# First layer's experts: an earlier flag for the branch, and later weight sums beside lone tiles

## Chip, cores and metric

The kernel runs on one core of a Trainium2 chip. The metric is the time of one execution on the device in microseconds, as the median of several runs. The engines are PE (TensorE, matrix products; its weight loads are listed as PEld), DVE (VectorE), ACT (ScalarE), POOL (GpSimd) and SP (SyncE, which here starts most DMAs). Each engine runs its own list of instructions in order and waits on semaphores for the others.

## What is computed

Two layers, each a graph convolution followed by a mixture of experts, on 3327 tokens of 256 features, in float32. `adj` is sparse: some 0.24% of its entries and the diagonal are not zero.

```python
# layer 0
x = x + relu(adj @ (layernorm(x) @ W) + b)
x = x + moe0(layernorm(x))      # 8 experts, 2 per token, hidden size 1024, relu
# layer 1
x = x + gnn1(layernorm(x))      # the 700 largest of tanh(adj * adj) in each row; tanh, relu
x = x + moe1(layernorm(x))      # 8 experts, 2 per token, hidden size 256, gelu; out = tokens + sum
```

For each chosen expert `e` of layer 0, a token gets `combine[e] * (relu(t @ W1[e].T + b1[e]) @ W2[e].T + b2[e])`.

## The kernel before

**Blocks of layer 0's experts.** Tokens are scattered into lists by expert, and the experts work through blocks: a pair is two tiles of 128 tokens of one expert, a lone tile is one. Blocks are numbered t = 0 to 29 and more if the data ask for it. Among t = 3 to 24 ("piped") the lone tiles are t = 12, 17 and 22. SP loads each block's tokens, weights and biases into a ring of six places, two for a block, so that a block's loads start about two blocks ahead of it.

**Seven products for eight.** A product of two by two halves is made with seven partial products instead of eight, after sums of the operands have been formed (the Strassen-Winograd scheme). This holds for pairs in both of an expert's products. The sums of the second product's weights `w2` are `t1, t2, t4, t3` (L1350, four VectorE operations of 128x512 that write the tile `gate`); those of its hidden activations are `s1, s2, s4, s3` (L1447, L1448, L1451, L1478). The sums of the first product's weights `w1` are made by POOL (L1532, L1533, L1535) and, one of them, by VectorE (L1515); those of its tokens by VectorE (L1544, L1547, L1548). A lone tile takes plain products.

**A period.** `piped_step(t)` works on two blocks at once: the first product of block t + 1 (`first_parts`, seven parts, products on L1586) alternates with the second product of block t (`second_parts` for a pair, products on L1435; `single_parts` for a lone tile, L1714). For i = 0 to 6 it lists part i of the first, then part i of the second, and between them what `after_first(i)` and `after_second(i)` hold. Part 2 of the first product adds a partial product into the hidden activations' quarter `c11` (L1609 on VectorE) and ACT applies bias and relu (L1594); part 3 ends with ACT's copy of a PSUM bank into `c12` (L1614), and part 5 accumulates into that bank, so it waits for the copy. L1622 adds into `c22`, and part 7 ends with the addition into `c12` (L1632); the relu of `c12` follows in the next period. In the next period the parts of block t + 1's second product follow: x_1, b_, z_1, x_2, z_2, x_3, q_. Their results are weighed and added to the output tile by VectorE (L1442, L1497). z_1 multiplies `s1` with `t1`, x_2 `s2` with `t2`, x_3 `s3` with `t3`, and q_ takes `t4`.

While period t runs, the four weight sums of block t + 1's second product (`nexts`) are listed one by one behind parts of block t, in the order that the dictionary gives:

```python
if i in (2, 3, 5, 6):
    nexts[{2: 0, 3: 1, 5: 3, 6: 2}[i]]()
```

**What sets the order on an engine.** The program is listed once; a scheduler then orders each engine's instructions: of those whose inputs it reckons ready, the one listed first goes first. `behind(x)` adds that what is listed inside it goes on its engine after the instruction x. The order is fixed when the program is built.

**The branch.** Before block 26 the kernel branches (`tc.If(first_usual > 0)`, L2233) on whether the usual counts of tokens hold. `usual()` (from L1140) forms the flag: one small PE product (L959), seven small VectorE operations (L961, L1147, L1148, L1150, L1154 twice, L1161), and then `nc.values_load`, in which each engine reads the flag from SBUF into a register (L1162). The call stands behind block 25, `layer0.step(late, place=...)`. A second such branch, in layer 1, forms its flag by the same function. In the usual arm SP loads outputs of earlier blocks (L1832), and blocks 26 to 29 follow. Blocks 25 and 26 are not piped: their weight sums are listed by `prepare` (L1353, behind the last operation on the output tile), the first product is L1385, and L1376 makes one of the sums of the activations.

Of the kernel before, what the change touches and what calls it, by code (L numbers as in the profile page):

```python
# [14 lines left out]
ALU = mybir.AluOpType  # L15
# [12 lines left out]
E = 8  # L28
# [7 lines left out]
TOPK = 700  # L36
# [28 lines left out]
FIXED = (4, 6)  # L65
# [14 lines left out]
BEGUN, FIRST_TILES, MORE_TILES = 12, 14, 22  # L80
# [48 lines left out]
def gnn_moe_two_layers(  # L129
# [24 lines left out]
    nc = tc.nc  # L154
# [31 lines left out]
    def blk(name, n):  # L186

        at = blk_places[name][blk_at[name] % len(blk_places[name])]
        blk_at[name] += 1
        return pad[:, at : at + n]  # L190
# [103 lines left out]
    def behind(instructions):  # L294

        if instructions and any(i is instructions[-1].ins for i in nc.cur_bb.bb.instructions):
            return tc.issue_after(instructions[-1].ins)
        return nullcontext()
# [657 lines left out]
    def tokens(routed, name="pl_cnt"):  # L956

        pc = pst.tile([P, E], F32, name="pc", tag="pt")
        nc.tensor.matmul(pc, lhsT=ones_sq, rhs=cum[:, routed, :], start=True, stop=True)  # L959
        cnt = work.tile([P, E], F32, name=name, bufs=1)  # L960
        nc.vector.tensor_copy(cnt, pc)  # L961
        return cnt
# [177 lines left out]
    def usual(covered, small, tier=None):  # L1140


        most = work.tile([P, 1], F32, name="pl_most", bufs=1)
        ok = work.tile([P, 1], F32, name="pl_ok", bufs=1)
        for i, (tiles, rows_) in enumerate(covered):
            cnt = tokens(tiles, "pl_first_cnt")
            nc.vector.tensor_tensor(cnt, cnt, rows_, ALU.is_gt)  # L1147
            nc.vector.tensor_reduce(most, cnt, AX.X, ALU.max)  # L1148
            if i == 0:
                nc.vector.tensor_scalar(ok, most, -1.0, 1.0, ALU.mult, ALU.add)  # L1150
            else:
                nc.vector.scalar_tensor_tensor(ok, most, 0.5, ok, ALU.is_le, ALU.mult)
        for number, limit in small:
            nc.vector.scalar_tensor_tensor(  # L1154
                ok[0:1, :], number, float(limit), ok[0:1, :], ALU.is_le, ALU.mult
            )
        if tier is not None:
            nc.vector.tensor_reduce(most, tier, AX.X, ALU.min)
            nc.vector.tensor_tensor(ok, ok, most, ALU.mult)
        flag = work.tile([P, 1], I32, name="pl_flag", bufs=1)  # L1160
        nc.vector.tensor_copy(flag, ok)  # L1161
        return nc.values_load(flag[0:1, 0:1], min_val=0, max_val=1)  # L1162

    def places(cnt, nb, base, size, starts_, n, at, table, own, aside):
# [51 lines left out]
    def experts(xlist, ys, group, fixed, n_hidden, func, w1T, b1, w2T, b2, copy, order_of_places, kept=None,  # L1216
# [49 lines left out]
        def groups_of(t):  # L1266
            return SG if t < EARLY or order[t - EARLY] < LATE_PAIRS else 1
# [64 lines left out]
        def halves(a, k, i):  # L1332
            return a[:, k * hc_n // 2 : (k + 1) * hc_n // 2, ts(i, P)]
# [169 lines left out]
                return [x_1, q_, b_, z_1, x_2, z_2, x_3]  # L1503
            return [x_1, b_, z_1, x_2, z_2, x_3, q_]

        weight_sums, owed_sums, owed_relu, begun_y = [], [], [], {}
        token_sums, hidden, ahead_sums = {}, {}, {}

        def quarter(w1, k, d):
            n = n_hidden // 2  # L1510
            return w1[:, d, k * n : (k + 1) * n]
# [39 lines left out]
        def first_parts(t):  # L1551

            _, _, w1, bb1, _, _ = loaded[t]
            xT = ready.pop(t)
            hT = blk("wide", hc_n * SB).rearrange("p (c b) -> p c b", b=SB)
            hidden[t] = hT
            hn = hc_n // 2

            if groups_of(t) < SG:
                def some(at):  # L1560
                    for hc in range(at, at + 2):
                        ps = psh.tile([P, P], F32, name="ps_h", tag="ph")
                        for c in range(DC):
                            last_product[:] = [nc.tensor.matmul(
                                ps, lhsT=w1[:, c, ts(hc, P)], rhs=xT[:, c, :], start=(c == 0),
                                stop=(c == DC - 1),
                            )]
                        last_hidden[:] = [nc.scalar.activation(
                            hT[:, hc, 0:P], ps, func, bias=bb1[:, hc : hc + 1]
                        )]  # L1570
                return [lambda at=at: some(at) for at in range(0, hc_n, 2)]

            s1, s2, s3, s4 = weight_sums[0:4]
            t1, t2, t3, t4 = token_sums.pop(t)
            a11, a12, a21, a22 = (quarter(w1, k, d) for k in range(2) for d in range(2))
            b11, b12, b21, b22 = (xT[:, d, ts(i, P)] for d in range(2) for i in range(2))
            c11, c12, c21, c22 = (halves(hT, k, i) for k in range(2) for i in range(2))
            ps = {}

            def bank(name, pool, tag):  # L1580
                ps[name] = pool.tile([P, hn, P], F32, name="ps_f", tag=tag)
                return ps[name]

            def multiply(out, a, b, first=True):
                for c in range(hn):
                    last_product[:] = [nc.tensor.matmul(  # L1586
                        out[:, c, :], lhsT=a[:, ts(c, P)], rhs=b, start=(first and c == 0),
                        stop=(c == hn - 1), skip_group_check=True,
                    )]

            def relu(k, i, src):
                for c in range(hn):
                    hc = k * hn + c
                    last_hidden[:] = [nc.scalar.activation(  # L1594
                        hT[:, hc, ts(i, P)], src[:, c, :], func, bias=bb1[:, hc : hc + 1]
                    )]

            def part1():
                multiply(bank("b", psh, "ph"), a11, b11)
                with behind(last_hidden):  # L1600
                    d = nc.scalar.copy(c11, ps["b"])
                with tc.issue_after(d.ins):
                    for q in owed_relu:
                        q()
                owed_relu.clear()

            def part2():
                multiply(bank("a", pst, "pt"), a12, b21)
                nc.vector.tensor_tensor(c11, c11, ps["a"], ALU.add)  # L1609
                relu(0, 0, c11)  # L1610

            def part3():
                multiply(ps["b"], s2, t2, False)
                nc.scalar.copy(c12, ps["b"])  # L1614

            def part4():
                multiply(bank("z", pst, "pt"), s1, t1)

            def part5():
                multiply(ps["b"], s3, t3, False)  # L1620
                nc.scalar.copy(c22, ps["b"])
                nc.vector.tensor_tensor(c22, c22, ps["z"], ALU.add)  # L1622

            def part6():
                multiply(ps["b"], a22, t4, False)
                relu(1, 0, ps["b"])
                with behind(last_hidden):
                    relu(1, 1, c22)

            def part7():  # L1630
                multiply(ps["z"], s4, b22, False)
                nc.vector.tensor_tensor(c12, c12, ps["z"], ALU.add)  # L1632
                owed_relu.append(lambda: relu(0, 1, c12))

            return [part1, part2, part3, part4, part5, part6, part7]

        def piped_step(t, late, place):
# [8 lines left out]
            sums = ahead_sums.pop(t, None)  # L1646
            nexts, weights_ = [nothing] * 4, [nothing] * 4
# [28 lines left out]
            def after_second(i):  # L1676
                if owed_sums and i in (1, 2):
                    owed_sums.pop(0)()
                if i in (2, 3, 5, 6):
                    nexts[{2: 0, 3: 1, 5: 3, 6: 2}[i]]()  # L1680

            for i in range(7):
                if first_[i]:
# [299 lines left out]
    with nc.allow_non_contiguous_dma("a few hundred elements"):  # L1983
# [8 lines left out]
    sums = const.tile([1, ng], F32, name="most_sums")  # L1992
    nc.vector.tensor_reduce(sums, pc.rearrange("o (n k) -> o n k", k=NCHUNK), AX.X, ALU.add)
    most_all = const.tile([1, 1], F32, name="most_all")
# [6 lines left out]
    late = plan(positive.rearrange("p n i k -> p (n i k)"))  # L2001
# [2 lines left out]
    layer0.steps_to(late, layer0.always - 5)  # L2004
    in_s = s.rearrange("p n d -> p (n d)")
    at = BEGUN * K * D
    layer0.step(late, place=in_s[:, at : at + DC * SB])

    first_usual = usual(
        [(BEGUN, late[4][:, E : 2 * E])],
        [(late[5][0:1, :], FIXED[0]), (most_all, TOPK + 0.5)],
    )
    before_branch, rows_before = layer0.state(), list(rows_written)
    begun_stats = (
        const.tile([P, BEGUN, 2], F32, name="begun_mv"), const.tile([P, BEGUN], I32, name="begun_rs")
# [213 lines left out]
    with tc.If(first_usual > 0) as arms:  # L2233
# [9 lines left out]
        with behind(last_y):  # L2243
# [10 lines left out]
        layer1.steps_to(late1, EARLY - 1)  # L2254
        layer1.step(late1, place=blk("xT_arms", DC * SB))
        baset, nbt = late1[4], late1[6]
        second_usual = usual(
            [(FIRST_TILES, baset[:, E : 2 * E]), (MORE_TILES, baset[:, 2 * E :])],
            [(late1[5][0:1, :], FIXED[1])],
            nbt[:, E : 2 * E],  # L2260
        )
        before_inner = layer1.state()
        with tc.If(second_usual > 0) as inner:
            layer1.know(2 * E)
# [213 lines left out]
```

## Time and profile before

| what | value |
|---|---|
| median of 8 runs | 1184.1 us (1181.87 to 1188.06) |
| the profiled execution | 1182.32 us, span 1180.6 us |
| granted TensorE clock | 0.988 |
| PE busy | 1131.5 us (96%) |
| VectorE busy | 923.1 us (78%) |
| ACT busy | 652.9 us (55%) |
| POOL busy | 395.7 us (34%) |

The profile is of one execution; the span runs from its first instruction to its last. A line of a timeline reads: start in us, duration in us, engine, source line, operation, output and inputs with sizes, count, and in brackets how long the engine had been idle and for whom it waited. A line of the list of waits reads: who waited for whom, us in total, times, longest. In the chain of waits, each piece is what the end of the execution hung on at that time. Matrix products overlap, and their ends are modelled: in the blocks, a product of 128x128 follows the one before it after 0.11 us while it is listed with 0.28.

### The profile page before, as it was taken

Reading aid. Unit: us, or ns where it says so; the run is one execution under the profiler, and the core shown is the slowest. Engines: PE = TensorE matmul, PEld = TensorE weight load, DVE = VectorE, ACT = ScalarE, POOL = GpSimd, SP = SyncE. Lnnn points to the kernel's source line nnn. Section 1 sums busy time; section 2 is a strip of 40 time slices with the busy share of each in tenths; the row PEclk is TensorE's granted clock in tenths of the full one; section 3 lists DMA queues with packets and bytes.
Section 4 is the critical chain, followed back from the end, with each engine's and each line's share of the span. In section 5 each row is a group of like instructions: output and inputs, shape, how many; then the busy total and the mean of one; then the engine's idle time right before and its main releaser. Section 6 shows DMA issues by size and latency. Waiting matters only on the chain.

```text
span 1180.6 us, 20682 instructions
## 1 busy us (share of the span) xinstructions
PE 1131.5 (96%) x6667; PEld 1010.7 (86%) x6667; DVE 923.1 (78%) x2728; ACT 652.9 (55%) x1309; POOL 395.7 (34%) x424
## 2 busy tenths in 40 slices
PE   8999999999999999999999999999999999988983
PEld 7888888888779999999998988888888888877862
DVE  6698999988868998888876669486798788784464
ACT  5699657550225655555553346989778683133331
POOL 2111331242434543535341110012444324554541
PEclk9999999999999999999999999999999999999997
DMA  9996638724465566676666955135644734557696
GB/s 349 183 266 264 242 122 249 254 78 165 139 203 191 195 229 229 192 251 214 226 231 234 360 195 215 59 116 192 221 145 170 262 122 130 181 166 232 202 295 221
DMA packets 123254, 241.77 MB, mean 205 GB/s; under 512 B 24528, under 2 KB 93184, under 8 KB 116224
## 3 DMA queue, kind: packets, MB, share of 16 engines
q1 hardware_dynamic: 108656, 205.59, 53.3%
q0 software_dynamic: 11200, 31.61, 7.4%
q10 hardware_dynamic: 3280, 3.15, 0.8%
q8 instruction: 55, 0.90, 0.3%
q14 instruction: 63, 0.52, 0.1%
HBM read 203.99 MB, written 36.33 MB: 204 GB/s over the span
## 4 chain that ended last, share of the span: by engine, by line
PE 82%; DMA 6%; DVE 6%; issue 3%; ACT 2%; POOL 1%; SPq 0%; ACTq 0%; DVEq 0%; POOLq 0%
PE ps_g L449 32%; PE ps_y L1435 10%; PE ps_h L1385 8%; PE ps_f L1586 8%; PE ps_y L1747 6%; PE ps_g L756 4%; DMA ring<-in_adjT 3%; PE ps_g L474 3%; PE ptb L1325 2%; PE ps_s L396 2%; PE ps_p L2063 2%; PE ps_o L485 2%; DMA ring<-ys 1%; DVE rt_product L819 1%; DMA x<-in_x 1%
## 5 line engine op out<-in xcount | busy, mean ns | idle before, releaser
L449 PE MATMUL ps_g<-ring,pad 128*128 128x256 f32 x1040 | 235.6, 381 | 1.3 <-DMA ring<-in_adjT 1.3
L449 PEld LDWEIGHTS ps_g<-ring,pad 128*128 128x128 f32 x1040 | 194.9, 190 | 26.9 <-DMA ring<-in_adjT 1.7
L946 POOL DMA_INDIRECT ys<-pad,index x114 | 118.2, 1037 | 196.0 <-DVE pad L1755 58.1
L449 PE MATMUL ps_g<-ring,s 128*128 128x256 f32 x780 | 176.8, 379 | 0.0
L459 DVE TENSOR_TENSOR ring<-ring,ring 128x768 f32<-128x768 f32 (+1 forms) x160 | 167.4, 1088 | 0.0
L449 PEld LDWEIGHTS ps_g<-ring,s 128*128 128x128 f32 x780 | 147.9, 190 | 19.9
L675 ACT ACTIVATE ring<-ring 128x3328 f32<-128x3328 f32 x54 | 160.1, 2976 | 1.2 <-DMA ring<-in_adjT 0.8
L946 POOL DMA_INDIRECT xlist<-xn,rt_idx x104 | 115.2, 1108 | 127.3 <-issue 39.5
L1925 ACT ACTIVATE sign<-ring,below 128x416 bf16<-128x416 f32 x208 | 133.4, 641 | 13.6 <-DMA ring<-in_adjT 7.7
L819 DVE SCALAR_TENSOR_TENSOR rt_product<-xn,gate 128x256 f32<-128x256 f32 x256 | 116.3, 454 | 15.1 <-ACT xn L361 5.6
L1393 ACT ACTIVATE pad<-ps_h,ring 128x256 f32<-128x256 f32 (+1 forms) x114 | 51.6, 455 | 133.9 <-PE ps_h L1385 94.3
L1385 PE MATMUL ps_h<-pad,ring 128*128 128x256 f32 (+1 forms) x512 | 113.9, 370 | 6.7 <-ACT pad L1329 4.1
L1385 PEld LDWEIGHTS ps_h<-pad,ring 128*128 128x128 f32 x512 | 90.3, 193 | 24.3 <-ACT pad L1329 5.6
L1594 ACT ACTIVATE pad<-pad,ring 128x128 f32<-128x128 f32 x216 | 69.0, 398 | 28.3 <-DVE pad L1609 26.8
L474 PE MATMUL ps_g<-ring,s 128*128 128x256 f32 x312 | 68.7, 380 | 3.9 <-ACT s L361 3.9
L474 PEld LDWEIGHTS ps_g<-ring,s 128*128 128x128 f32 x312 | 58.9, 190 | 12.4 <-ACT s L361 4.4
L756 PE MATMUL ps_g<-s,ring 128*128 128x256 f32 x312 | 69.0, 380 | 0.0
L756 PEld LDWEIGHTS ps_g<-s,ring 128*128 128x128 f32 x312 | 58.8, 190 | 7.9
L1442 DVE SCALAR_TENSOR_TENSOR pad<-ps_y,ring,pad 128x128 f32<-128x128 f32 x138 | 47.1, 344 | 15.6 <-PE ps_y L1435 14.2
L929 POOL COPY xn<-rt_w 128x4 f32<-128x4 f32 x26 | 4.6, 200 | 163.2 <-DVE rt_w L892 163.2
L1586 PE MATMUL ps_f<-xn 128*128 128x128 f32 x432 | 56.9, 276 | 2.0 <-ACT pad L1614 2.0
L1532 POOL TENSOR_TENSOR xn<-ring 128x512 f32<-128x512 f32 x18 | 27.9, 1553 | 90.0 <-DMA ring<-in_f_w1T 83.3
(287 smaller groups left out, 2139.7 us busy)
## 6 DMA issues: line engine op xcount, KB each, us to landing
ring<-in_adjT SPq DMA_DIRECT2D x50, 1664.0 KB
ring<-in_f_w1T SPq DMA_DIRECT2D x30, 1024.0 KB
ring<-in_f_w2T SPq DMA_DIRECT2D x30, 1024.0 KB
ring<-xlist SPq DMA_DIRECT2D x52, 258.0 KB
ring<-in_f_w SPq DMA_DIRECT2D x36, 256.0 KB
ring<-ys SPq DMA_DIRECT2D x12, 512.0 KB
ring<-in_f_b SPq DMA_DIRECT2D x34, 128.0 KB
xlist<-h2T SPq DMA_DIRECT2D x16, 257.0 KB
```

The costliest lines, as they stand in the source:

```text
L449: nc.tensor.matmul(ps, lhsT=b[:, c, :], rhs=a[:, c, :], start=(first and c == 0), stop=(c == CJ - 1), skip_group_check=not first,)
L459: nc.vector.tensor_tensor(out[:, part, :], out[:, part, :], other[:, part, :], ALU.add)
L474: nc.tensor.matmul(sums[pan][c], lhsT=s[:, j, ts(c, P)], rhs=piece(pan, j // CJ)[:, j % CJ, :], start=(j == 0), stop=(j == NT - 1),)
L675: last_pass[:] = [nc.scalar.activation(a, a, f)]
L756: nc.tensor.matmul(banks_[it], lhsT=piece(pan, k)[:, c, ts(it, P)], rhs=s[:, j, :], start=(j == 0), stop=(j == NT - 1),)
L819: nc.vector.scalar_tensor_tensor(product, xn, 1.0, gate[:, e, :], ALU.mult, ALU.mult, accum_out=sc[:, e : e + 1],)
L946: d = nc.gpsimd.indirect_dma_start(out=a[:, :], out_offset=bass.IndirectOffsetOnAxis(ap=index, axis=0), in_=rows_, in_offset=None,)
L1385: last_product[:] = [nc.tensor.matmul(ps, lhsT=w1[:, c, ts(hc, P)], rhs=xT[:, c, :], start=(c == 0), stop=(c == DC - 1),)]
L1435: last_product[:] = [nc.tensor.matmul(ps, lhsT=a[:, c, :], rhs=b[:, c, :], start=(first and c == 0), stop=(c == hc_n // 2 - 1), skip_group ...
L1586: last_product[:] = [nc.tensor.matmul(out[:, c, :], lhsT=a[:, ts(c, P)], rhs=b, start=(first and c == 0), stop=(c == hn - 1), skip_group_c ...
L1747: last_product[:] = [nc.tensor.matmul(ps, lhsT=hT[:, hc, ts(g, P)], rhs=w2[:, hc, :], start=(hc == 0), stop=(hc == hc_n - 1),)]
L1925: nc.scalar.activation(sign, piece(pan, k)[:, :, ts(i, GROUP)], AF.Sign, bias=below, accum_out=positive[:, pan, i, k : k + 1],)
```

## The change

It has two parts. First, `usual()` returns the flag's tile, and a new function `is_set()` reads it into the registers. For layer 0 the flag is formed ahead of block 25 and read where it was read before, behind it. For layer 1 both calls stand where the one stood.

Second, in the period of a lone tile (`sums` is empty there) the four weight sums `nexts` are no longer listed behind parts 3, 4, 6 and 7, but all behind part 7, and on VectorE's list after `last_sum`, the addition into `c12` that part 7 of `first_parts` ends with (L1632). In the periods of pairs nothing changes.

```diff
@@ usual
         flag = work.tile([P, 1], I32, name="pl_flag", bufs=1)
         nc.vector.tensor_copy(flag, ok)
+        return flag
+
+    def is_set(flag):
         return nc.values_load(flag[0:1, 0:1], min_val=0, max_val=1)
@@ first_parts
             def part7():
                 multiply(ps["z"], s4, b22, False)
-                nc.vector.tensor_tensor(c12, c12, ps["z"], ALU.add)
+                last_sum[:] = [nc.vector.tensor_tensor(c12, c12, ps["z"], ALU.add)]
                 owed_relu.append(lambda: relu(0, 1, c12))
@@ piped_step
             def after_second(i):
                 if owed_sums and i in (1, 2):
                     owed_sums.pop(0)()
-                if i in (2, 3, 5, 6):
+                if sums and i in (2, 3, 5, 6):
                     nexts[{2: 0, 3: 1, 5: 3, 6: 2}[i]]()
+                if not sums and i == 6:
+                    with behind(last_sum):
+                        for q in nexts:
+                            q()
@@ before the branch of layer 0
-    layer0.step(late, place=in_s[:, at : at + DC * SB])
-    first_usual = usual(
+    usual_flag = usual(
         [(BEGUN, late[4][:, E : 2 * E])],
         [(late[5][0:1, :], FIXED[0]), (most_all, TOPK + 0.5)],
     )
+    layer0.step(late, place=in_s[:, at : at + DC * SB])
+    first_usual = is_set(usual_flag)
@@ before the branch of layer 1
-        second_usual = usual(
+        second_flag = usual(
             [(FIRST_TILES, baset[:, E : 2 * E]), (MORE_TILES, baset[:, 2 * E :])],
             [(late1[5][0:1, :], FIXED[1])],
             nbt[:, E : 2 * E],
         )
+        second_usual = is_set(second_flag)
```

More of the change, by code (lines that the diff above doesn't have):

```diff
@@ L1504, in second_parts @@
             return [x_1, b_, z_1, x_2, z_2, x_3, q_]
-        weight_sums, owed_sums, owed_relu, begun_y = [], [], [], {}
+        weight_sums, owed_sums, owed_relu, last_sum, begun_y = [], [], [], [], {}
         token_sums, hidden, ahead_sums = {}, {}, {}
```

## Prediction

> **What bounds the kernel now.** I read the page first. TensorE is busy 96% of the span at a granted clock of 0.99, so a microsecond is won only where PE stands still. The second view is the list of PE's waits from 440 to 660 us, the stretch of the pipelined blocks of layer 0 and of the branch:
>
> ```profile
> PE   1131.5 (96%) x6667; PEld 1010.7 (86%) x6667; DVE 923.1 (78%) x2728; ACT 652.9 (55%) x1309; POOL 395.7 (34%) x424
> ```
> ```profile
> PE ps_h L1385 <- DVE pl_flag L1161: 2.8, 1, 2.8
> PE ps_f L1586 <- ACT pad L1614: 2.0, 3, 1.1
> PE ps_y L1435 <- DVE xnT L1447: 0.8, 3, 0.4
> ```
>
> These are all of PE's waits there: one at the branch, and two in or just after each of the three lone tiles (t = 12, 17, 22). The change aims at the first and second rows; the third is the one it can make worse. Third, the chain of waits around the branch:
>
> ```profile
> 639.88 0.05 PE pc L959
> ...
> 641.62 0.17 DVE pl_flag L1161
> 641.78 0.88 issue
> 642.66 2.49 PE ps_h L1385 x10
> ```
>
> PE has nothing to do from its last product (next one possible at 639.71) to 642.66, 2.95 us: the flag's small operations stand behind the block's last VectorE work (L1442, until 640.52), and then every engine reads the flag and branches (0.88). Last, VectorE's timeline in the first lone period:
>
> ```profile
> 474.07 0.68 DVE L1350 TENSOR_TENSOR gate<-ring 128x512 f32<-128x512 f32 x1
> ...
> 475.67 0.68 DVE L1350 TENSOR_TENSOR gate<-ring,gate 128x512 f32<-128x512 f32 x1
> 476.27 0.68 DVE L1350 TENSOR_TENSOR gate<-ring 128x512 f32<-128x512 f32 x1
> 476.87 0.68 DVE L1350 TENSOR_TENSOR gate<-ring,gate 128x512 f32<-128x512 f32 x1
> 477.47 0.68 DVE L1609 TENSOR_TENSOR pad<-pad,ps_f 128x512 f32<-128x512 f32 x1
> 481.79 0.69 DVE L1622 TENSOR_TENSOR pad<-pad,ps_f 128x512 f32<-128x512 f32 x1 [3.65 <-ACT pad L1621]
> ...
> 485.76 0.68 DVE L1632 TENSOR_TENSOR pad<-pad,ps_f 128x512 f32<-128x512 f32 x1
> 486.36 0.15 DVE L1409 TENSOR_TENSOR index<-index,positive 128x2 int32<-128x2 f32 x1
> 486.43 0.34 DVE L1442 SCALAR_TENSOR_TENSOR pad<-ps_y,ring,pad 128x128 f32<-128x128 f32 x1
> 487.08 0.69 DVE L1609 TENSOR_TENSOR pad<-pad,ps_f 128x512 f32<-128x512 f32 x1 [0.31 <-PE ps_f L1586]
> 487.79 1.12 DVE L1447 TENSOR_TENSOR xnT<-pad 128x512 f32<-128x512 f32 x1
> ```
>
> The four weight sums (L1350) run ahead of L1609, so c11 is late, then ACT's relu, then its copy L1614, for which PE waits. After that VectorE idles 3.65 us. But behind L1632 it has no room: the table by stages gives it 12.70 busy of 13.00 us from 487 to 500 and 12.93 of 13.00 from 500 to 513, and z_1 starts at 488.96, 0.05 after L1447.
>
> **The flag.** Seven small operations (0.15 to 0.19 us each, 640.44 to 641.78 or 1.34 us in all) and one product (0.17) move ahead of block 25. They have their inputs long before. On VectorE they can delay block 25's weight sums, which end at 629.57 and are first needed by a product at 634.35, and L1376, after which VectorE idles 2.73 us; so 1.34 us is covered (uncovered it would cost at most 1.34). No DMA moves; SP, POOL and ACT only meet their flag reads without a wait, and SP's first transfers in the arm still wait for the block's last scatter, issued at 641.40. What stays on PE is reading and branching: 641.81 to 642.66, 0.85 us. At the second branch PE reads the flag while products are queued, and at 1124.65 a read and eight register steps begin while LDWEIGHTS issue on until 1125.5, so PE's queue reaches at least 0.85 us ahead there. I take 0.2 us left of the 2.95: a gain of 2.75; the ends are 2.95 (fully hidden) and 2.1 (0.85 in the open). VectorE, which also restarts earlier, does so after its last L1442, before it is needed.
>
> [...] The queue of this trace shows no more than about ten instructions ahead.
>
> **The sums behind the activations' sums, first lone period.** What is won: L1609 no longer stands behind three of the sums. It waits for its product, 475.98 + 0.10 = 476.08, ends 476.75; the relu's first three and a part (1.19) let L1614 end at 478.53; PE reaches part5 at 478.48 + 0.86 = 479.34 instead of 479.98. Won: 0.64 (0.56 and 1.29 in the other two, by the same rows: 540.67 - 540.11, 601.80 - 600.51).
>
> What it costs: L1632 now comes earlier too, and behind it the four sums go in one piece, since nothing listed before them is left. The same construction in block 25 shows the order (two L1353, a third, an index operation, the fourth, 626.96 to 629.57). Forward from part5 at 479.34: L1622 481.15, three token sums to 482.82, L1719 to 483.26, L1720 blocked by POOL's L1532 until 484.35, L1632 484.35 to 484.95. Then 4 x 0.60 of sums + 0.33 (L1409, L1442) + 0.60 (L1609) + 0.60 (L1447) = 3.95: 488.90 without POOL. That is already the 488.91 at which L1447 ends now: all that was won is spent. And POOL's own sums of 1.27 us fall into it. What they do to such an operation the trace shows:
>
> ```profile
> 497.03 2.20 DVE L1350 TENSOR_TENSOR gate<-ring 128x512 f32<-128x512 f32 x1
> ```
> ```profile
> 497.38 1.29 POOL L1535 TENSOR_TENSOR xn<-ring,xn 128x512 f32<-128x512 f32 x1
> ```
>
> The weight sum ends 0.56 after POOL's. So L1533 (to 485.57) holds the first sum 0.6, and L1535, from 486.7 behind a scatter, holds the third 1.2: L1447 ends at 490.7, z_1 starts at 490.75 instead of 488.96, **+1.8**. Second lone period, the same way: 551.35 instead of 549.66, **+1.7**. Third, where L1632 gains 2.4 us because PE had waited 1.12 there: 611.65 instead of 610.93, **+0.7**. Behind z_1 VectorE is full for two more blocks (13.17 us from L1447 to L1447, PE's own 12.94), so nothing is caught up. Sum +4.2. Ends for each period: 1.2 less, if POOL's L1535 lets the sums pass, 0.3 more, if b_'s L1442 goes ahead of L1447 too; so +0.6 to +5.1.
>
> [...]
>
> **Sum.** -2.75 + 4.2 = +1.45 us against the profiled execution (1182.3, span 1180.6, 1.7 around it; 1.8 under the median of the runs). On the median of 1184.1: 1185.5, inside the 0.2% (2.4 us) that a measurement of this kernel can tell from no change. Ends: +0.6 - 2.95 = -2.35 and +5.1 - 2.1 = +3.0.
>
> **Rivals.** (1) *The sums find room.* If L1442, L1609 and L1447 go ahead of the sums, z_1 is not delayed and the three waits on L1614 vanish: -0.64 - 0.56 - 1.29 = -2.5, with the flag -5.25: 1178.9. For: VectorE idles 3.65 us in that period now, and z_1 needs only the first sum. Against: idle time lies before L1632, and the sums may not start there any more. (2) *The arm is not at hand.* PE's 2.1 us of standing before the read (639.71 to 641.81) may have covered the fetch of the arm's instructions. Now PE arrives at once; if the fetch takes over 0.85 us it shows, and at 2.1 the flag gains only 0.65: +4.2 - 0.65 = +3.55, 1187.7. For: one branch on PE, at 1159.71, lasts 3.96 us. Against: that one jumps; both branches that fall into an arm take 0.08. (3) *The first half does nothing*, because the sums were ready too late anyway: then L1609 would not stand behind them; the timeline excludes it.
>
> **How the numbers follow.** The forecast's case 0.58: its centre +1.45 with ends -2.35 to +3.0, widened by shifts of the rest of the order, puts 0.23 over +2.4, 0.32 between, 0.03 under -2.4. Rival 1: 0.25, all faster. Rival 2: 0.17, slower. Together faster 0.28, same 0.32, slower 0.40. The range goes from 1178.8, through the middle of rival 1, to 1188.6, past rival 2 and its spread of 1; about 0.13 and 0.04 are left out. The forecast's own range is 1181.7 to 1187.1.
>
> **What would show it.** The wait on pl_flag gone and PE's gap at the branch under 0.5 us; no wait of PE on L1614; the four L1350 in one piece after L1632; PE's waits on L1447 grown from 0.8 us to some 7; POOL's L1535 inside the sums. Wrong if L1447 stands ahead of the sums (rival 1), or PE idles over 1 us between the branch and its next product (rival 2).

## The result and the profile after

The kernel after takes 1188.9 us (median of 24 runs), the kernel before 1183.8 us beside it (66 runs). The ratio is 1.0048, interval 1.0033 to 1.0063, so the change costs 5.7 us (3.9 to 7.5); the two medians lie 5.1 us apart. The forecast was 1185.5 us, +1.45; the range ended at 1188.6, just below the result.

The profiled execution after has a span of 1194.3 us at a clock of 0.979; with 1196.0 us it is one of the kernel's longest. Some 5 us of its distance to the one before arise before 350 us, in code that the change leaves as it was; this does not belong to the change. From 475 us on the two differ by +8.4 us, which can be followed piece by piece. First the page and the list of PE's waits in the stretch of the blocks and of the branch (who waits for whom: us in total, times, longest):

```profile
PE 1140.4 (95%) x6667; PEld 1019.6 (85%) x6667; DVE 925.3 (77%) x2728; ACT 652.7 (55%) x1309; POOL 394.5 (33%) x424
```
```profile
PE ps_y L1438 <- DVE xnT L1450: 9.6, 4, 3.0
PE ps_f L1589 <- DMA ring<-in_f_w1T: 0.8, 1, 0.8
```

(Lines after L1160 have moved by 3, those behind the period's code by 7.) The waits on `pl_flag` and on L1614 are gone. In their place PE waits four times for s1 (L1450, which was L1447): in the periods behind the three lone tiles, 8.2 us together, and in block 28, 1.3 us. VectorE's timeline in the first of these periods, and what POOL does there:

```profile
489.61 0.68 DVE L1635 TENSOR_TENSOR pad<-pad,ps_f 128x512 f32<-128x512 f32 x1
490.20 1.97 DVE L1353 TENSOR_TENSOR gate<-ring 128x512 f32<-128x512 f32 x2
492.10 2.21 DVE L1353 TENSOR_TENSOR gate<-ring,gate 128x512 f32<-128x512 f32 x1
...
494.56 0.67 DVE L1353 TENSOR_TENSOR gate<-ring,gate 128x512 f32<-128x512 f32 x1
495.16 0.67 DVE L1612 TENSOR_TENSOR pad<-pad,ps_f 128x512 f32<-128x512 f32 x1
...
496.02 0.89 DVE L1450 TENSOR_TENSOR xnT<-pad 128x512 f32<-128x512 f32 x1
```
```profile
489.75 1.27 POOL L1536 TENSOR_TENSOR xn<-xn,ring 128x512 f32<-128x512 f32 x1
...
492.46 1.29 POOL L1538 TENSOR_TENSOR xn<-ring,xn 128x512 f32<-128x512 f32 x1
494.85 1.52 POOL L1535 TENSOR_TENSOR xn<-ring 128x512 f32<-128x512 f32 x1 [1.10 <-DMA ring<-in_f_w1T]
```

VectorE's order is the predicted one but for one operation: the four sums stand in one piece behind L1635, POOL's sums fall inside them, and s1 comes last, with a second L1445 ahead of it as well. PE's order has changed too. The kernel before has eight products of the next block in front of z_1, the kernel after has sixteen, so eight products (1.0 us) run before the wait that came after it:

```profile
487.70 1.06 PE L1586 MATMUL ps_f<-xn 128*128 128x128 f32 x8
488.96 1.16 PE L1435 MATMUL ps_y<-gate,xnT 128*128 128x128 f32 x8 [0.20 <-DVE xnT L1447]
```
```profile
491.99 1.95 PE L1589 MATMUL ps_f<-xn 128*128 128x128 f32 x16
496.97 2.07 PE L1438 MATMUL ps_y<-gate,xnT 128*128 128x128 f32 x8 [3.04 <-DVE xnT L1450]
```

What the prediction did not have stands in the table of stretches, which gives for each its length, busy time (and count) of PE, PEld, DVE, ACT and POOL, then the granted clock, the DMA share and GB/s:

```profile
493.22:496.64 3.42, 0.71 (x7) 0.52 (x5) 3.42 (x7) 0.77 (x3) 2.24 (x3) 1.00 1.01 338
496.64:500.05 3.41, 3.08 (x13) 3.04 (x14) 3.38 (x5) 0.98 (x3) 1.41 (x1) 0.50 0.29 102
500.05:503.46 3.41, 3.41 (x32) 3.41 (x32) 3.41 (x9) 1.08 (x2) 0.00 (x0) 1.00 0.02 5
```

PE stands idle for 3.04 us up to 496.97, and then its clock is 0.50 for 3.41 us: 13 products where the next stretch has 32. Behind the second lone tile it is at half for 6.83 us (561.49 to 568.32), behind the third not at all. Product by product against the kernel before, the three periods cost 3.6, 5.9 and 0.6 us, the branch gains 2.95, and block 28 gives 1.3 back. In the second period 0.8 us is the wait for `in_f_w1T` in the list above, which two later profiles of the kernel after do not have.

### The profile page after: what moved, and what is told of

It is laid out like the page before. It is cut to its first block, busy times and chain, and to the rows that moved or that the text cites. A ratio compares the mean times of both kernels' runs of the same rounds, so it can differ in the third digit from the quotient of the medians.

```text
span 1194.3 us, 20678 instructions
## 1 busy us (share of the span) xinstructions
PE 1140.4 (95%) x6667; PEld 1019.6 (85%) x6667; DVE 925.3 (77%) x2728; ACT 652.7 (55%) x1309; POOL 394.5 (33%) x424
## 5 line engine op out<-in xcount | busy, mean ns | idle before, releaser
L1388 PE MATMUL ps_h<-pad,ring 128*128 128x256 f32 (+1 forms) x512 | 117.3, 378 | 7.5 <-ACT pad L1332 4.1
L474 PEld LDWEIGHTS ps_g<-ring,s 128*128 128x128 f32 x312 | 60.1, 194 | 11.5 <-ACT s L361 3.1
L1445 DVE SCALAR_TENSOR_TENSOR pad<-ps_y,ring,pad 128x128 f32<-128x128 f32 x138 | 47.2, 345 | 17.0 <-PE ps_y L1438 15.8
L1438 PE MATMUL ps_y<-gate,xnT 128*128 128x128 f32 x352 | 49.6, 288 | 9.6 <-DVE xnT L1450 9.6
L1535 POOL TENSOR_TENSOR xn<-ring 128x512 f32<-128x512 f32 x18 | 29.8, 1658 | 84.7 <-DMA ring<-in_f_w1T 78.0
```

The lines of the kernel that those rows point to most:

```text
L474: nc.tensor.matmul(sums[pan][c], lhsT=s[:, j, ts(c, P)], rhs=piece(pan, j // CJ)[:, j % CJ, :], start=(j == 0), stop=(j == NT - 1),)
L1388: last_product[:] = [nc.tensor.matmul(ps, lhsT=w1[:, c, ts(hc, P)], rhs=xT[:, c, :], start=(c == 0), stop=(c == DC - 1),)]
L1438: last_product[:] = [nc.tensor.matmul(ps, lhsT=a[:, c, :], rhs=b[:, c, :], start=(first and c == 0), stop=(c == hc_n // 2 - 1), skip_group ...
```

## The experiments

They ran in three groups, each beside runs of the kernel before: 1166.9 us in the first, 1185.9 in the second, 1167.2 in the third. Only ratios within a group are compared. "The clock's part" is (1 - granted clock) x span, the mean over a kernel's runs; it also counts half-clock time in which PE waited anyway.

| kernel | group | ratio to before (interval) | us | clock's part (before) |
|---|---|---|---|---|
| e1_flag | 1 | 0.9993 (0.9978 to 1.0009) | -0.8 | 9.7 (10.5) |
| e2_sums | 1 | 1.0071 (1.0046 to 1.0095) | +8.3 | 13.4 (10.5) |
| e3_c11 | 1 | 0.9983 (0.9963 to 1.0004) | -2.0 | 10.7 (10.5) |
| e4_filler | 1 | 1.0036 (1.0022 to 1.0050) | +4.2 | 9.2 (10.5) |
| p_before | 2 | 1.0002 (0.9980 to 1.0025) | +0.2 | 16.9 (15.7) |
| p_after | 2 | 1.0037 (1.0019 to 1.0055) | +4.4 | 18.2 (15.7) |
| e5_best | 2 | 0.9962 (0.9938 to 0.9985) | -4.5 | 15.0 (15.7) |
| e6_flag_loads | 2 | 0.9940 (0.9921 to 0.9960) | -7.1 | 14.7 (15.7) |
| e7_no_pool | 3 | 0.9964 (0.9946 to 0.9982) | -4.2 | 10.0 (11.0) |
| e8_c11_only | 3 | 0.9978 (0.9958 to 0.9999) | -2.6 | 11.5 (11.0) |
| e9_filler14 | 3 | 1.0026 (1.0009 to 1.0043) | +3.0 | 8.8 (11.0) |
| p_after2 | 3 | 1.0062 (1.0043 to 1.0082) | +7.2 | 14.7 (11.0) |

**Each part alone.** The flag (after, with the sums back in their places), and the sums (before, with `last_sum` and `behind` as in the change):

```diff
# e1_flag, against after
-                if sums and i in (2, 3, 5, 6):
+                if i in (2, 3, 5, 6):
                     nexts[{2: 0, 3: 1, 5: 3, 6: 2}[i]]()
-                if not sums and i == 6: ...
# e2_sums, against after
-        return flag
-    def is_set(flag):
         return nc.values_load(...)      # usual() called and read behind block 25, as before
```

> The flag formed ahead of block 25, the weight sums where they were. Theory (the gain at the branch is partly handed back): PE's gap of 2.95 us at the branch goes whole, but PE stands about 1.3 us in front of block 28's first products of the second half, because VectorE's weight sums of block 28 wait for its w2, which SP's queue brings behind three large loads of outputs. Net -1.65 us, ratio 0.9986, and VectorE's L1353 sums near 680 us show a wait for in_f_w2T of about 1.3 us. Rival (the hand-back belongs to the sums, not to the flag): -2.95 us, 0.9975, no such wait. Rival (the flag itself costs, by fetching the arm's code or by block 25's later sums): PE's gap at the branch stays over 1 us and the ratio is 1.000 or more.

> The weight sums of lone tiles behind the addition into c12, the flag where it was. Theory (delay of s1 and a halved clock behind it): PE's wait on L1614 goes and waits on s1 of 2 to 3 us appear in the three periods; behind those of some 3 us the granted clock is 0.5 for 3.4 us or more, which costs 1.7 us for each 3.4 us; together +7 to +10 us, ratio 1.006 to 1.0085; PE's gap at the branch stays at 2.8. Rival (only the waits count, the halved clock comes and goes with the run as it does in the kernel before): +4 to +5 us, 1.0035 to 1.004, and no half-clock stretch that follows the lone tiles' gaps. Rival (the slower time lies elsewhere, before block 12 or in layer 1): 1.000 to 1.002 with the same gaps.

With the flag alone PE has no idle time over 0.12 us at the branch, but 1.45 us in front of block 28's z_1. VectorE's waits and its timeline there:

```profile
DVE gate L1356 <- DMA ring<-in_f_w2T: 1.4, 1, 1.4
```
```profile
657.04 1.29 DVE L1356 TENSOR_TENSOR gate<-ring 128x512 f32<-128x512 f32 x2 [1.37 <-DMA ring<-in_f_w2T]
...
660.59 5.76 DVE L1849 TENSOR_TENSOR x<-x,s 128x1024 f32<-128x1024 f32 x5
...
666.94 0.69 DVE L1450 TENSOR_TENSOR xnT<-pad 128x512 f32<-128x512 f32 x1
```

Block 28's `w2` has not landed when VectorE, now 2.95 us earlier, wants it; the additions of earlier outputs (L1849) follow without a break, and s1 is late by the same amount. So the hand-back belongs to the flag, against the first rival; and with nothing left of the gap at the branch the second has fallen too. Net by the profile -2.95 + 1.45 = -1.5; measured -0.8 (-2.6 to +1.1), which agrees with the -1.65 expected but does not prove a gain. The sums alone cost 8.3 us (5.4 to 11.1), as the theory said and above the rival's 4 to 5.

**What the lateness of s1 is made of.** In group 3 POOL's three sums in a lone tile's period were left out, with the order on PE and VectorE as in the kernel after; the next block then works with stale sums, so only the times count:

```diff
# e7_no_pool, against after
-                    weights_ = sum_weights(t + 2)
+                    weights_ = sum_weights(t + 2) if sums else [nothing] * 2 + sum_weights(t + 2)[2:3] + [nothing]
```

> The kernel after, in which POOL leaves out its three sums of w1 (L1535, L1536, L1538) that belong to a lone tile's period: nothing else is moved, the block behind reads stale sums. Theory (the four sums and what follows take 4 us by themselves, and POOL's operations in the same microseconds hold VectorE's up by 2 to 4 us more): VectorE's four L1353 run at 0.60 us each, and PE's waits on s1 go from 2 to 3 us in a period to 0 to 1; with no half-clock stretch behind them; 6 to 8 us faster than the kernel after, ratio to the kernel before 0.997 to 0.999. [...]

> The kernel after, unchanged, beside the three others on the same chip: 1.0035 to 1.0055 by both theories, with waits on s1 of 2 to 3 us in the three periods and in most executions one to three half-clock stretches behind them.

VectorE's timeline of the first period, without POOL's sums (e7_no_pool), and with them (p_after2):

```profile
477.90 0.69 DVE L1635 TENSOR_TENSOR pad<-pad,ps_f 128x512 f32<-128x512 f32 x1
478.50 1.29 DVE L1353 TENSOR_TENSOR gate<-ring 128x512 f32<-128x512 f32 x2
479.71 0.69 DVE L1353 TENSOR_TENSOR gate<-ring,gate 128x512 f32<-128x512 f32 x1
...
482.10 0.68 DVE L1450 TENSOR_TENSOR xnT<-pad 128x512 f32<-128x512 f32 x1
```
```profile
479.72 0.67 DVE L1635 TENSOR_TENSOR pad<-pad,ps_f 128x512 f32<-128x512 f32 x1
480.31 1.78 DVE L1353 TENSOR_TENSOR gate<-ring 128x512 f32<-128x512 f32 x2
482.02 2.20 DVE L1353 TENSOR_TENSOR gate<-ring,gate 128x512 f32<-128x512 f32 x1
...
485.93 1.64 DVE L1450 TENSOR_TENSOR xnT<-pad 128x512 f32<-128x512 f32 x1
```

From L1635's start to s1's end it is 4.88 us without POOL's sums and 7.85 with them. The 2.97 between are 0.49 in the first two sums, 1.51 in the third and 0.96 in s1 itself, which POOL's L1535 for the next block (485.75) now hits. This is one period. Over all of them the same stretch takes 4.87 to 4.88 us in e7_no_pool, and 6.1 to 9.3 in the nine lone periods of after, p_after and p_after2 (7.3 on the mean): POOL's part is 1.3 to 4.4 us, 2.4 on the mean. PE's waits on s1 in the lone periods vanish altogether:

```profile
PE ps_y L1438 <- DVE xnT L1450: 1.5, 1, 1.5
PE ps_y L1438 <- DVE pad L1445: 0.5, 2, 0.3
```
```profile
PE ps_y L1438 <- DVE xnT L1450: 10.5, 4, 3.4
```

The one left of 1.5 is block 28's. Before 0.9964, p_after2 1.0062: leaving POOL's sums out is worth 11.4 us. That is more than the 6 to 8 expected: the clock's part falls with the waits, by 4.7 us, and VectorE comes to the sums earlier (L1727, held to 1.21 us by POOL in p_after2, takes 0.35). So it is not VectorE's own work alone that makes s1 late.

**The clock.** Idle products (their result is overwritten) fill PE's gap ahead of z_1, ten in group 1, fourteen in group 3:

```diff
# e4_filler (10) and e9_filler14 (14), against after, in z_1
+                if t - 1 in piped and groups_of(t - 1) < SG:
+                    for _ in range(14):
+                        nc.tensor.matmul(ps_z, lhsT=ident, rhs=ident, start=True, stop=True)
                 multiply(ps_z, s1, t1)
```

> The kernel after, and in the three periods behind a lone tile ten more products of 128x128 (identity by identity) ahead of the first product that needs s1, into a bank that is overwritten afterwards: they keep PE at work in its gap and change nothing in the result. Theory (a stretch of half clock follows a gap of about 3 us): the gap of PE is cut by about 1.1 us where it stands, the products behind start at the same time as before, and with the gap under 2.2 us the clock stays at 1.0, so the kernel is 3 to 5 us faster than the kernel after: ratio to the kernel before 1.000 to 1.002. Rival (the clock does not depend on the gap): no change against the kernel after, 1.004 to 1.006, and stretches of 0.5 as before. Rival (the products stand in the way of those behind): slower than the kernel after.

> The kernel after, with fourteen products of 128x128 (identity by identity, into a bank that is overwritten) ahead of the first product that needs s1 in the three periods. Theory (the half-clock stretches come from PE's idle stretches): no half-clock stretch from 470 to 650 us, the time that the clock takes away some 3 to 4 us less than in the kernel after on the same chip, and the kernel 2 to 4 us faster than that one. Rival (the clock does not follow PE's work): the same as the kernel after or slower.

```profile
480.66 3.29 PE L1479 MATMUL ps_y<-ident 128*128 128x128 f32 x28
484.13 1.16 PE L1438 MATMUL ps_y<-gate,xnT 128*128 128x128 f32 x8 [0.19 <-DVE xnT L1450]
```

Each product shows as two matmuls in the trace (28 for fourteen), and fourteen take 3.29 us (I had reckoned 1.1 us for ten; they took 2.40) and close the gap to 0.19. They do not bring z_1 forward. The eight products that p_after2 has in front of z_1 stand behind it here, and PE has no useful product for 3.4 to 3.5 us ahead of z_1 in each of the three periods, where p_after2 has none for 2.7 to 3.4. (s1 itself ends 6.13 us after the start of the addition into `c12`, not 7.85, since POOL's sums fall elsewhere in this execution.) But the first z_1 product group takes 1.16 us where p_after2's takes 2.08:

```profile
487.62 2.08 PE L1438 MATMUL ps_y<-gate,xnT 128*128 128x128 f32 x8 [3.36 <-DVE xnT L1450]
```

No stretch of half clock is left between 470 and 650 us. The kernel is 4.3 us faster than p_after2 (1171.05 against 1175.32; by the means 4.1, give or take 1.8), and the clock's part falls from 14.7 to 8.8. So keeping PE at work for nothing wins 4 us, though PE's time without useful work has not become shorter: that is what the halved clock costs there. The +3.0 us left (1.1 to 5.0) is in the main the time ahead of z_1, less what is won at L1614 and at the branch. The ten products of e4_filler also left no half-clock stretch, with gaps of 0.4 to 1.1 us; but 1.0036 (1.0022 to 1.0050) missed the 1.000 to 1.002 expected, and as the kernel after did not run in that group, its gain can't be read.

**The kernels before and after, profiled beside the others.**

> The kernel before, unchanged, for a profile on the chip of these runs. Theory (PE's clock is set for stretches of 3.41 us on a grid of its own; a stretch in which PE works less than half is followed by one at 0.5): ratio 1.000; the waits on pl_flag, L1614 and L1447 as in the first profile, 2.8, 2.0 and 0.8 us; a half-clock stretch behind the branch's gap in some executions and not in others, as the gap of 2.8 us falls on the grid. Rival (the clock depends on the gap's length alone): either always or never behind a gap of 2.8 us.

> The kernel after, unchanged, on the chip of these runs and with the granted clock of every run. Theory (two terms: s1 late by 2 to 3 us in three periods, and a half-clock stretch of 3.41 us behind those in which PE works less than half of the stretch before): the time that the clock takes away, (1 - granted clock) x span, is some 3 us more than in the kernel before on the mean, the rest of the time some 3.5 us more, together ratio 1.0045 to 1.006. Rival (the clock plays no part): the clock's part is the same in both, the ratio no more than 1.003.

The second group repeats the result at 1.0037, below the 1.0045 to 1.006 expected; the third, at 1.0062, lies above its 1.0035 to 1.0055. In the second group the means differ by 5.1 us: 2.5 in the clock's part and 2.5 in the rest, where 3 and 3.5 were expected. The profile of p_before shows that the kernel before pays the clock's price too. Its stretches around the branch:

```profile
640.31:643.73 3.42, 0.99 (x5) 0.92 (x6) 2.37 (x11) 0.00 (x0) 1.83 (x2) 1.00 0.21 77
643.73:647.14 3.41, 3.41 (x10) 2.67 (x9) 1.79 (x9) 0.95 (x2) 0.00 (x0) 0.50 0.50 135
```

and the same gap in the first profile of before, where it fell across two stretches and cost nothing:

```profile
637.71:641.12 3.41, 2.17 (x21) 1.99 (x19) 1.80 (x8) 0.00 (x0) 0.96 (x1) 1.00 0.00 0
641.12:644.53 3.41, 1.87 (x9) 1.52 (x9) 2.46 (x8) 0.47 (x1) 0.96 (x1) 1.00 0.21 77
644.53:647.95 3.42, 3.42 (x17) 2.75 (x17) 1.60 (x8) 1.90 (x4) 0.00 (x0) 1.00 0.70 249
```

The 171 products behind the branch take 29.31 us in p_before and 27.71 in the first profile: the half-clock stretch costs 1.6 us.

**Another place, and the order of the loads.** The sums behind the addition into c11 (part 2), where VectorE had idle time, with the flag (e3) and without (e8); and block 28's loads listed ahead of the loads of earlier outputs, with the flag alone (e6) and with both (e5):

```diff
# e3_c11, e5_best (against after); e8_c11_only has the same place and the flag of before
-                nc.vector.tensor_tensor(c11, c11, ps["a"], ALU.add)
+                last_sum[:] = [nc.vector.tensor_tensor(c11, c11, ps["a"], ALU.add)]
...
-                if not sums and i == 6:
+                if not sums and i == 1:
                     with behind(last_sum):
# e5_best, e6_flag_loads
         output_loads.clear()
+        layer0.load(late)
         for yt, t, n in begun:
             load_outputs(yt, ys0, t, n, written, "read0")
```

> Both parts, but in lone tiles' periods the weight sums stand behind the addition into c11 (part 2) instead of the one into c12 (part 7), where VectorE stood idle for 3.65 us. Theory (what costs is that s1 stands behind the sums; the place and not the move itself): PE waits neither on L1614 nor on s1, the clock stays up through blocks 12 to 23, and the time is -2.5 (three waits) -1.65 (flag) = -4 us against the kernel before, ratio 0.9965. Rival (the sums hold VectorE up wherever they stand, s1 is late again for want of room): s1 late by 1 to 2 us in each period, ratio 1.000 to 1.003. Rival (the three waits on L1614 were hidden anyway or come back later): only the flag's gain, 0.9985.

> The kernel before, with the weight sums of lone tiles' periods behind the addition into c11; the flag as it was. Theory (the three waits on L1614, about 2 us together, go and nothing comes in their place but 0.2 to 0.9 us on s1): -1 to -2.5 us, ratio 0.998 to 0.999. Rival (the waits were hidden anyway or come back with s1): 1.000 to 1.001.

> As the kernel with the sums behind the addition into c11, and in the usual arm block 28's loads listed ahead of the three loads of earlier outputs. Theory: w2 of block 28 is there when VectorE wants it, PE's gap of 1.3 us in block 28 goes, and the time is 1.3 us under that kernel's: -3.3 to -5 us against the kernel before, ratio 0.996 to 0.997. Rival (the loads of outputs come too late instead and VectorE's additions of them, L1853 in the kernel after, hold up the same sums): a gap of 1 us or more stays near 665 us and the ratio is 0.998.

> The flag alone, and block 28's loads listed ahead of the three loads of earlier outputs. Theory (the flag is worth its 2.8 to 2.95 us, and the order of the loads gives back 1.3): -2.9 us, ratio 0.9975, and no gap of PE near 665 us. Rival (the flag is worth less than its gap, as PE is held up by something else behind): -0.5 to -1.5 us, 0.999, as the flag alone measured at 0.9993.

PE's waits in e3_c11, and in e6_flag_loads from 440 to 690 us:

```profile
PE ps_y L1438 <- DVE xnT L1450: 2.7, 4, 1.3
```
```profile
PE ps_f L1589 <- ACT pad L1617: 2.7, 3, 1.2
PE ps_y L1438 <- DVE xnT L1450: 1.2, 2, 0.6
```

Behind c11 nothing waits on the copy any more and s1 costs 0.3, 0.2 and 0.9 us (1.3 is block 28's): the place decides, not the move. The sums there win 2.6 us (0.1 to 4.9) alone; with the flag, -2.0 (-4.3 to +0.5) was measured where -4 was expected, near the interval's end. By its time alone e3 does not part the theory from its last rival (only the flag's gain, 0.9985); PE's waits do, and e8, if by little. With block 28's loads first, its gap is gone in both kernels, and VectorE's wait on `in_f_w2T` with it; L1849's operands cause no new one. Both versions are faster than either kernel: -4.5 us (1.8 to 7.4) and -7.1 us (4.7 to 9.4). e5 lies where it was expected, e6 beyond its -2.9. That e6, without the new place, is not slower than e5, and that it wins more than its 2.95 us of gap and 1.7 us for one half-clock stretch explain, stays open: it has 6 runs, the intervals of the two overlap, and the one profiled is the longest of the six.

## Why the prediction was wrong

**The flag at the branch: right, but not to the end.** Reading and branching left nothing in the open: gain 2.95, the upper end of the term. The hand-back was missing: the step "No DMA moves", with SP's first transfers in the arm waiting for the block's last scatter (1.0 us in the first profile of before, 11.1 in that of after), was true and its consequence not drawn. If the loads stay and the work comes 2.95 us earlier, the load with the least margin becomes the wait. It was block 28's w2: PE waited 1.3 to 1.7 us in block 28 in the profiles that form the flag early and keep the order of the loads. The term should have been some -1.5 instead of -2.75.

**The sums in one piece behind L1632: right.** So was the gain at L1614: 0.74, 0.66 and 1.39 us in the first pair of profiles, where 0.64, 0.56 and 1.29 were forecast. So was, nearly, "488.90 without POOL": from L1632's start that is 4.55 us, and without POOL's sums it took 4.88, as the second L1445 went ahead of s1 (the prediction had this among its ends; its parts also add up to 3.93, not 3.95). PE's waits on s1 were then gone.

**POOL's part: the mechanism right, the size not.** The term had 0.6 + 1.2 = 1.8 us in the first period; by e7_no_pool and p_after2 it is 2.97, and 1.3 to 4.4 over all the profiles of the kernel after. The missing piece is mostly the last one: once s1 is late, POOL's sum for the next block, 1.27 us, falls into it as well (0.96). In the third period the prediction let L1632 gain 2.4 us because PE had waited 1.12 us there; that wait was 0.30 in p_before, so +0.7 was the reading of one execution. PE waits there 2.2 to 2.8 us for s1 in the profiles of the kernel after. The end of 1.2 less, with POOL's third sum letting VectorE's pass, no profile of the kernel after showed: POOL's part was 1.3 us at the least. An earlier start did not spare VectorE's sum either: in p_after2 L1353 started at 482.02, POOL's L1538 at 482.37, and again the former took 2.20 us and the latter its usual 1.29.

**The step that failed most: no term for the clock.** The sum took a PE wait at its own length. It cost more: a wait that left PE working less than 41% of one stretch of 3.41 us was followed by a stretch at half clock in every profile, by estimate half of 3.41 or 1.7 us for work that PE limits (1.6 measured behind p_before's branch). The trace of before had this in view (a gap of 2.51 us at 1050.63 and a clock of 0.5 from 1050.75 on); I read only the mean of 0.99. By e9_filler14 this is some 4 us of the kernel after's 7.2 in its group.

Put together for the first pair of profiles, term by term: the three periods cost 10.1 us instead of 4.2, the branch won 2.95 instead of 2.75, and block 28 took 1.3 instead of nothing, in all +8.4 instead of +1.45. Of the 10.1, 4.7 are the halved clock (half of the 9.3 us that PE worked in the three stretches at 0.50), 0.8 the wait for `in_f_w1T`, and 4.6 what the forecast had at 4.2. That these two lie so close is luck in part: in the first period s1 ended 3.0 us later than in the kernel before, counted from the period's start, not 1.8, but PE had eight more products (1.0 us) to work on until then, which the prediction did not have. By the runs the change costs 5.7, 4.4 and 7.2 us in the three comparisons, somewhat less than in this pair of profiles; what makes up that difference stays open.

**The rivals.** "The sums find room" did not happen in this place, and did in the place of e3_c11, but for 0.9 us in the third period. "The arm is not at hand" fell: no idle time at the branch. "The first half does nothing" fell too: the waits on L1614 are gone.

## What to carry to other kernels

A wait of the bounding engine is to be priced with what follows it, here a half-clock stretch of 1.7 us, and the list of clock stretches read before the mean. Work that is put in one piece onto an engine can meet all of another engine's work there, as the sums met POOL's here (2.97 us in the first period): sum the other's operations over the whole piece, and once more over the lateness they cause. When a wait is removed, look whether the loads behind it move with it; here they stayed, and the smallest margin among them limited the gain.

## What the runs showed of the hardware

PE's clock changed on a grid of 3.413 us: in the first profile of before its changes lie 317.44, 3.41, 723.63, 3.41, 13.65, 3.41 and 92.16 us apart, 93, 1, 212, 1, 4, 1 and 27 times that. The grid's place differed from execution to execution (a boundary 2.86 us behind the span's start there, 1.70 in the first profile of after). Over the 14 profiles of this case, every stretch at full clock in which PE was busy for less than 41% was followed by one at half (36 of 36), none of those with 47% or more (0 of 4620), and 7 of 11 between. This leaves out the stretch ahead of each execution's closing part, where PE does nothing more and the clock is at half; of these 14, one with 48.6% (e7_no_pool, at 1138.10) was followed by half clock, so the upper bound is not quite sharp. So a gap's place counts as much as its length. In e2_sums a gap of 2.28 us halved the clock and one of 2.86 us, which fell across two stretches, did not:

```profile
551.61:555.03 3.42, 1.30 (x11) 1.31 (x11) 3.39 (x8) 1.75 (x5) 0.32 (x1) 1.00 1.04 376
555.03:558.44 3.41, 3.41 (x17) 3.41 (x17) 3.41 (x4) 0.18 (x1) 2.57 (x2) 0.50 0.53 170
613.05:616.46 3.41, 1.93 (x18) 1.74 (x16) 3.41 (x7) 0.16 (x1) 0.59 (x1) 1.00 0.94 315
616.46:619.88 3.42, 2.04 (x17) 2.04 (x18) 3.39 (x7) 1.75 (x5) 0.00 (x0) 1.00 1.09 368
619.88:623.29 3.41, 3.41 (x32) 3.41 (x32) 3.02 (x7) 1.07 (x3) 0.00 (x0) 1.00 0.11 37
```

Idle time of some 2 us within one stretch (59% of 3.413) was thus always enough, and in e5_best a gap of 3.84 us, split between two stretches that were busy for 45% and 43%, was not.

A stretch at half clock was followed by another where PE waited in it too: the five in which it was busy for 83% or less were, the 43 with 87% or more were not.
